# First layer: the first 512 tokens' chain moved ahead, transposes of the identity on TensorE meanwhile, and the last 512 tokens normalised on GpSimd

## The chip, the cores and the metric

The kernel runs on one core of a Trainium2 chip. It is written in Bass and Tile, as one program with instruction queues for TensorE (PE in the profile, its weight loads PEld), VectorE (DVE), ScalarE (ACT), GpSimd (POOL) and SyncE (SP, which only issues transfers here). The metric is the device time of one execution in microseconds (us), and the time of a kernel is the median of its runs.

## The reference, cut to what matters

Two layers work on 2048 tokens of width 128 in f32. Each is a layer normalisation, an attention and a gate with a residual:

```
xn = layernorm(x)                      # mean, variance, 1e-5
s  = L0_attn(xn)                       # 16 heads of width 8, relu attention
g  = silu(L0_ffn(xn))                  # 255 routed tokens go through a small block
x  = x + s * g
...                                    # layer 1: causal softmax attention, gated feed-forward
```

The relu attention of layer 0 is

```
qkv = xn @ w_qkv                       # 128 -> 16 heads x (q, k, v) of 8
w   = relu(q @ k^T / sqrt(8));  attn = w / (sum(w) + 1e-6)
out = attn @ v @ w_out + b_out;  y = xn + out;  layernorm(y) * gamma + beta
```

The routed block scores every token with `xn @ router_w`, takes the 255 highest of 2048, and works on these alone. All of it starts from the layer normalisation of the 2048 tokens, which the change touches.

## The kernel before, in words

*Tokens.* The 2048 tokens lie as 16 blocks of 128 partitions in `xin` (lines 82 to 86). They are handled in four groups of 512, and 512 is also the width of a chunk of queries. `normalised(i)` (lines 874 to 903) is a generator for one group. Its first part takes the statistics of four blocks on DVE (two instructions for each block), adds 1e-5 and takes the root on ACT; its second part forms the reciprocal root on DVE (a reciprocal and four small operations), normalises four blocks into `xne` on DVE (line 895), transposes them on TensorE into one PSUM bank (`transposed`, line 102) and copies the bank to `xnT` on ACT (line 104).

*Projections.* `project` (line 783) makes four copies of the heads' rows for one group of heads: a product `xnT` x weights, written as one 512-wide f32 product, which shows as two matmuls; a copy `high` on ACT rounded to fp32r; and a DVE instruction (line 793) that writes the rounded value or the remainder, by row, into `kT` or `qT`. This is called the split below. `spread` (line 807) does the same for all 16 heads at once, into two tiles, `high` and `low`, with one PSUM bank, tag "x", that is freed by DVE's split (line 819). These tiles go to `kT` and through DRAM (`rows`) to the other head groups by transfers on SP (`key_group`, `kept`, `group`; lines 825 to 839). `values(i)` (line 862) makes four products for v, which show as eight matmuls, and one copy on ACT.

*Steps.* The attention runs over 256 steps, n = 0 to 255: four chunks of queries, four groups of four heads, sixteen blocks of keys. `scores(n)` (line 942) makes four products side by side in the rows of the array, each into a PSUM bank of tag "s" (six of them), and four relus out of them, on ACT (line 956) or DVE (line 958), whichever `work` holds to be less loaded; `work` is a running sum of estimated microseconds for both engines. `products(n)` (line 961) comes two steps later and multiplies the relus with the values, four f32 products of two matmuls each. A step on TensorE is `scores(n)`, then what the step before left for later, then `products(n - 2)`, then one piece of other work: the piece that the table `due` (line 1066) has for the step, or else the next piece of the generator `others`, which runs the routed block first.

*Order.* TensorE, ACT and DVE issue in the order in which the program emits their instructions (`tc.manual_schedule`, line 89). GpSimd and SP are ordered by the scheduler of Tile, by emission order among what it takes to be ready. `begin` (line 907) is the part before the steps: the first parts of groups 0 and 1, the rest of group 0, `keys(0)`, the rest of group 1, `queries()`, the statistics of group 2, `values(0)`. Groups 2 and 3 are finished by `more` in steps 1 and 4.

*GpSimd.* It makes the identity matrix `ident`, re-lays the weights of the projections (lines 127 to 147), and then the constants of the routed block (lines 167 and 247 to 317): iotas, masks, zeros. Their emission stands in the first piece of the routed block, in step 10, but the scheduler puts them as early as their inputs allow. One of them, `nothing`, is 256 KB of zeros, which SP writes four times to the DRAM tile `back` (line 304). `w_qkv`, `w_out` and `router_w` are loaded on the ACT queue, all other inputs on SP's.

## Time and profile before

| | |
|---|---|
| median of 3 runs | 1464.82 us (1464.33 to 1466.9) |
| the profiled execution | 1466.11 us, its span 1464.4 us |
| busy: PE, DVE, ACT, POOL | 1412.4, 1057.6, 955.1, 329.8 us |
| mean granted TensorE clock | 0.993 |
| first transposes of tokens (line 102) | 11.27 us |
| scores of steps 0, 5, 12 (line 948) | 19.23, 36.04, 55.58 us |
| constants on POOL (lines 167 to 317) | 6.67 to 13.48 us, one more at 13.98 |

Times inside the profile count from the start of the span. A row of a timeline reads: start, length, engine, line, operation, what it writes and from what, the number of instructions merged, and in brackets how long the engine was idle before it and what ended that. A row of a table of stretches gives, behind the length, the busy time of PE, PEld, DVE, ACT and POOL with the number of instructions begun, then the granted TensorE clock as a share of the full one, the busy share of the DMA engines, and GB/s.

### The profile page before, as it was taken

The page shows a single profiled execution, that of the slowest core. Times are in us where ns is not written, and L with a number is a line of the kernel's source. Part 1 is how long each engine was busy: PE and PEld are TensorE (multiplying, and loading weights), DVE is VectorE, ACT ScalarE, POOL GpSimd, SP SyncE. Part 2 cuts the span into 40 slices and gives each one's busy share as a digit, 9 for nine tenths or more (in the row PEclk, how much of TensorE's full clock was granted, in tenths as well). Part 3 has the DMA queues.
Part 4 walks back from the last instruction along what each step waited for, and adds up shares of the span by engine and source line. Part 5 has one row for each costly group of instructions (what it writes and reads, how often), then busy time and mean ns, then how long its engine had stood idle before and what let it go on. Part 6 is the DMA issues. An engine that isn't in the chain of part 4 may idle for free.

```text
span 1464.4 us, 27046 instructions
## 1 busy us (share of the span) xinstructions
PE 1412.4 (96%) x10250; PEld 863.5 (59%) x10250; DVE 1057.6 (72%) x1905; ACT 955.1 (65%) x2055; POOL 329.8 (23%) x457
## 2 busy tenths in 40 slices
PE   5999999999999999999999999999999999999997
PEld 2222332322222476777777777777777777777775
DVE  6588788788888485577677677667667667776765
ACT  4587788788888467656556556556656656655653
POOL 2001000150000132322322222332242242242310
PEclk9999999999999999999999999999999999999999
DMA  4342001101000310010001000010010001000000
GB/s 122 122 83 69 12 12 32 51 26 42 19 20 4 99 30 15 15 30 15 16 19 24 17 16 15 17 29 16 15 30 15 15 15 30 15 15 15 16 23 23
DMA packets 33986, 44.49 MB, mean 30 GB/s; under 512 B 7360, under 2 KB 22080, under 8 KB 33856
## 3 DMA queue, kind: packets, MB, share of 16 engines
q1 hardware_dynamic: 33040, 41.45, 11.6%
q8 instruction: 81, 1.33, 0.4%
q0 software_dynamic: 384, 1.05, 0.3%
q14 instruction: 49, 0.40, 0.1%
q10 hardware_dynamic: 432, 0.26, 0.1%
HBM read 15.95 MB, written 8.17 MB: 16 GB/s over the span
## 4 chain that ended last, share of the span: by engine, by line
PE 61%; ACT 2%; DVE 1%; issue 1%; DVEq 0%; ACTq 0%
PE t L1458 18%; PE z L1508 17%; PE t L1688 16%; PE m L1568 2%; PE m L1396 2%; PE m L1361 2%; PE m L1411 2%; PE m L1553 2%; ACT p L1492 1%; ACT pt L1695 1%; PE m L1290 0%; DVE tops L1479 0%; PE m L1308 0%; DVE t L1478 0%; DVE pt L1695 0%
## 5 line engine op out<-in xcount | busy, mean ns | idle before, releaser
L1479 DVE TENSOR_REDUCE tops<-t 128x1 f32<-128x1024 f32 (+4 forms) x320 | 334.6, 1062 | 63.1 <-PE t L1458 56.0
L956 ACT ACTIVATE rt<-t 128x512 f32<-128x512 f32 x597 | 315.4, 605 | 64.7 <-PE t L948 63.3
L1695 ACT COPY pt<-t 128x512 f32<-128x512 f32 (+3 forms) x359 | 163.3, 518 | 267.1 <-PE t L1688 266.0
L1492 ACT ACTIVATE p<-t,tops 128x1024 f32<-128x1024 f32 (+7 forms) x384 | 331.0, 881 | 2.9 <-DVE tops L1479 2.4
L958 DVE TENSOR_SCALAR rt<-t 128x512 f32<-128x512 f32 x427 | 275.7, 684 | 70.0 <-PE t L948 64.9
L1458 PE MATMUL t<-k,q 128*128 128x512 f32 (+4 forms) x1280 | 316.6, 390 | 7.4 <-ACT p L1492 7.4
L964 PE MATMUL t<-rt,va 128*9 128x512 f32 x2048 | 270.0, 600 | 4.3 <-ACT part L980 4.3
L1688 PE MATMUL t<-ident,p 128*128 128x128 f32 x2176 | 269.9, 274 | 3.0 <-ACT x L1382 1.4
L1508 PE MATMUL z<-pt,v 128*64 128x256 f32 (+1 forms) x2304 | 270.0, 376 | 0.5 <-ACT zs L1702 0.5
L1458 PEld LDWEIGHTS t<-k,q 128*128 128x128 f32 x1280 | 219.1, 189 | 79.5 <-issue 36.1
L1688 PEld LDWEIGHTS t<-ident,p 128*128 128x128 f32 x2176 | 243.6, 141 | 25.4 <-ACT pt L1695 4.9
L1508 PEld LDWEIGHTS z<-pt,v 128*64 128x64 f32 x2304 | 152.6, 137 | 87.7 <-issue 23.0
L948 PEld LDWEIGHTS t<-qT,kT 32*128 32x128 f32 x1024 | 63.0, 182 | 180.8 <-ACT rt L956 108.6
L1695 DVE COPY pt<-t 128x512 f32<-128x512 f32 (+3 forms) x289 | 163.5, 605 | 2.6 <-PE z L1508 1.5
L948 PE MATMUL t<-qT,kT 32*128 32x512 f32 x1024 | 152.6, 499 | 2.7 <-ACT rt L956 1.9
L1478 DVE TENSOR_TENSOR t<-t,mask_q 128x128 f32<-128x128 f32 (+1 forms) x192 | 65.0, 339 | 86.4 <-PE t L1458 78.0
L1384 POOL CAST q<-x 64x512 fp32r<-64x512 f32 x60 | 36.6, 610 | 372.7 <-ACT x L1382 339.9
L1492 ACT ACTIVATION_READ_ACCUMULATOR p<-t,tops 128x1 f32 x384 | 84.2, 219 | 0.0
L1558 DVE TENSOR_TENSOR zs<-zs,m 128x512 f32<-128x512 f32 (+1 forms) x49 | 32.7, 675 | 65.8 <-PE m L1553 65.7
L1386 POOL TENSOR_TENSOR k<-x,k 64x512 fp32r<-64x512 f32 x60 | 76.4, 1273 | 4.6
L1386 POOL TENSOR_TENSOR q<-x,q 64x512 fp32r<-64x512 f32 x60 | 76.2, 1270 | 4.6
L1384 POOL CAST k<-x 64x512 fp32r<-64x512 f32 x60 | 36.6, 609 | 158.6 <-ACT x L1382 156.8
(316 smaller groups left out, 991.8 us busy)
## 6 DMA issues: line engine op xcount, KB each, us to landing
q<-q SPq DMA_DIRECT2D x64, 256.0 KB
qT<-spread SPq DMA_DIRECT2D x60, 64.0 KB
kT<-spread SPq DMA_DIRECT2D x48, 64.0 KB
spread<-high SPq DMA_DIRECT2D x8, 256.0 KB
spread<-low SPq DMA_DIRECT2D x8, 256.0 KB
rows<-xne SPq DMA_DIRECT2D x1, 1048.0 KB
xin<-in_x SPq DMA_DIRECT2D x4, 256.0 KB
back<-nothing SPq DMA_DIRECT2D x4, 256.0 KB
```

The lines of the kernel that those rows point to most:

```text
L948: nc.tensor.matmul(t, kT[rows, g, kb * P : (kb + 1) * P], qTs[qc, g][rows, :], start=True, stop=True,)
L956: nc.scalar.activation(rt, t, AF.Relu, scale=scale)
L958: nc.vector.tensor_scalar(rt, t, scale, 0.0, ALU.mult, ALU.max)
L964: nc.tensor.matmul(acc[32 * j : 32 * j + HD0 + 1, :], va[:, kb, 4 * g + j, :], r[j], start=(kb == 0), stop=(kb == NC - 1),)
L1384: nc.gpsimd.tensor_copy(high, x[half(e), :])
L1386: nc.gpsimd.tensor_tensor(low, x[half(e), :], high, ALU.subtract)
L1458: nc.tensor.matmul(flat[:, at_x : at_x + y - x], q[:, part, c4 * P : (c4 + 1) * P], k[:, x:y], start=(part == 0), stop=(part == 1),)
L1479: nc.vector.tensor_reduce(M[pr, c // 4][:, h, c % 4, es], x, axes, ALU.max, negate=True)
L1492: nc.scalar.activation(dst, x, AF.Exp, bias=M[pr, c // 4][:, h, c % 4, e : e + 1], accum_out=Z[pr, c // 4][:, h, c % 4, e : e + 1],)
L1508: nc.tensor.matmul(l1.z[half(e), slot, lo:2, :], V[pr, h][:, kb, half(e)], pts[e][:, kb, lo:2, :], start=(kb == 0), stop=(kb >= n0 - 1), s ...
L1688: nc.tensor.transpose(t[:, k + b, :], x[lo + b], ident)
L1695: copy(dst, t)
```

## The change

Loads: the first 512 tokens are fetched in two transfers, then `w_qkv`, then the other three groups, all on SP, where `w_out` and `router_w` are now issued too. The queries' weights are re-laid ahead of the keys'.

`normalised` is taken apart into `stats` (any blocks of a group), `root`, `normal` (on a given engine) and `turn` (transposes and copy). `fill(n)` transposes the identity n times into a PSUM bank that nobody reads. `begin` is 36 such transposes, the chain of group 0, six more transposes, queries before keys, and group 1; the key split of the first 128 keys comes by itself, ahead of that of the other 384. Only one block of group 2 has its statistics taken here.

In the steps, group 2's other statistics and normalisation follow the keys of group 1, group 3's statistics come in step 2, and group 3 is normalised by GpSimd. The table `due` is filled anew: steps 0 to 11 are all taken, so the routed block's first piece, with GpSimd's constants, comes in step 12; `rwb`, the broadcast router weight, is made there too. The reads of head group 1's keys follow the new order. GpSimd issues in emission order from `begin` to step 16.

```diff
-    for i in range(NQ):
-        nc.sync.dma_start(out=xin[:, 4 * i : 4 * i + 4, :], in_=xsrc[:, 4 * i : 4 * i + 4, :])
+    for i in range(2):
+        nc.sync.dma_start(out=xin[:, 2 * i : 2 * i + 2, :], in_=xsrc[:, 2 * i : 2 * i + 2, :])
...
-    nc.scalar.dma_start(
+    nc.sync.dma_start(
         out=w_qkv.rearrange("p g j t d -> p (g j t d)"), in_=a["w_qkv"]
     )
+    for i in range(1, NQ):
+        nc.sync.dma_start(out=xin[:, 4 * i : 4 * i + 4, :], in_=xsrc[:, 4 * i : 4 * i + 4, :])
...
-    for t, dst in ((1, w_k), (0, w_q)):
+    for t, dst in ((0, w_q), (1, w_k)):
...
-    nc.scalar.dma_start(out=w_out, in_=a["w_out"])
+    nc.sync.dma_start(out=w_out, in_=a["w_out"])
...
-    nc.scalar.dma_start(out=router_w, in_=a["router_w"])
+    nc.sync.dma_start(out=router_w, in_=a["router_w"])
...
-    nc.gpsimd.tensor_copy(rwb, router_w.to_broadcast([P, P]))
...
     yield
 
+    nc.gpsimd.tensor_copy(rwb, router_w.to_broadcast([P, P]))
     tok = rb.tile([P, KSEL], BF16, name="tok")
...
-    def project(dst, w, i, low):
+    def project(dst, w, i, low, cuts=(0, 512)):
...
-        nc.scalar.copy(high, t)
+        parts = [slice(*x) for x in zip(cuts, cuts[1:])]
+        for x in parts:
+            nc.scalar.copy(high[:, x], t[:, x])
         work.add(a=0.6, d=0.75)
-        return lambda: nc.vector.scalar_tensor_tensor(dst, high, low, t, ALU.mult, ALU.add)
+
+        def split(x):
+            nc.vector.scalar_tensor_tensor(
+                dst[:, x], high[:, x], low, t[:, x], ALU.mult, ALU.add
+            )
+
+        return [lambda x=x: split(x) for x in parts]
...
+    def stats(i, ks):
         st = small.tile([P, 4, 6], F32, tag="ln_st", name="ln_st")
+        for k in ks:
+            nc.vector.bn_stats(st[:, k, :], xin[:, 4 * i + k, :])
+            nc.vector.bn_aggr(moment[:, i, k, :], st[:, k, :])
+
+    def root(i):
...
+        nc.vector.tensor_scalar(v, moment[:, i, :, 1], 1e-5, None, ALU.add)
+        nc.scalar.activation(y, v, AF.Sqrt)
+        inverse[i] = v, y
+
+    def normal(i, engine):
...
         nc.vector.reciprocal(y, y)
+        engine.tensor_tensor(t, y, y, ALU.mult)
+        engine.tensor_tensor(t, t, v, ALU.mult)
+        engine.tensor_scalar(t, t, -0.5, 1.5, ALU.mult, ALU.add)
+        engine.tensor_tensor(r, y, t, ALU.mult)
+        for k in range(4):
+            c = 4 * i + k
+            engine.tensor_scalar(
+                xne[:, c, 0:D], xin[:, c, :], moment[:, i, k, 0:1], r[:, k : k + 1],
                 ALU.subtract, ALU.mult,
             )
...
+    def fill(n):
+
+        t = bank([P, 4, P], "s")
+        for k in range(n):
+            nc.tensor.transpose(t[:, k % 4, :], ident, ident)
 
     def begin():
 
-        next(tokens[0])
-        next(tokens[1])
-        next(tokens[0])
-        k = keys(0)
-        next(tokens[1])
-        q = queries()
-        k()
-        next(tokens[2])
-        q()
-        values(0)
-        work.a, work.d = 0.0, 3.0
+        fill(36)
+        stats(0, range(4))
+        root(0)
+        stats(1, range(2))
+        normal(0, nc.vector)
+        turn(0)
+        fill(6)
+        stats(1, range(2, 4))
+        root(1)
+        (q,) = queries()
+        k_first, k_rest = keys(0, (0, P, 512))
+        stats(2, range(1))
+        normal(1, nc.vector)
+        turn(1)
+        q()
+        k_first()
+        values(0)
+        k_rest()
+        work.a, work.d = 0.0, 1.0
+
+    def more(i):
+        turn(i)
+        work.add(a=0.6)
+        if i == 2:
+            return lambda: moments_used(3, nc.gpsimd)
+
+    def moments_used(i, engine):
+        root(i)
+        normal(i, engine)
+        work.add(a=0.2, d=0.5)
 
     def more_keys():
-        return keys(1)
+        (k,) = keys(1)
+
+        def later():
+            k()
+            stats(2, range(1, 4))
+            moments_used(2, nc.vector)
+            work.add(d=2.8)
+
+        return later
+
+    def no_more():
+        work.add(d=1.7)
+        return lambda: stats(3, range(4))
...
-        0: (more_keys,), 1: (more, 2), 2: (all_keys, 2), 3: (more_values, 1), 4: (more, 3),
-        5: (all_keys, 3), 6: (more_values, 2), 7: (all_keys, 1), 8: (all_queries, 0),
-        9: (more_values, 3), 11: (all_keys, 0),
+        0: (more_keys,), 1: (no_more,), 2: (more_values, 1), 3: (more, 2),
+        4: (all_keys, 2), 5: (more_values, 2), 6: (more, 3), 7: (all_keys, 3), 8: (all_keys, 0),
+        9: (all_queries, 0), 10: (more_values, 3), 11: (all_keys, 1),
...
-        9: (2, 1), 10: (3, 1), 12: (1, 1), 14: (0, 1),
+        9: (2, 1), 11: (3, 1), 12: (0, 1), 14: (1, 1),
...
+    first = ExitStack()
+    first.enter_context(tc.manual_schedule(engines={mybir.EngineType.Pool}))
     begin()
     for n in range(n_steps + 2):
+        if n == 16:
+            first.close()
```

## The prediction

> **What bounds the kernel now.** I read the page first: shares, slices, chain.

> ```profile
> PE 1412.4 (96%) x10250; PEld 863.5 (59%) x10250; DVE 1057.6 (72%) x1905; ACT 955.1 (65%) x2055; POOL 329.8 (23%) x457
> ...
> PE   5999999999999999999999999999999999999997
> ...
> PE 61%; ACT 2%; DVE 1%; issue 1%; DVEq 0%; ACTq 0%
> ```

> TensorE is busy 96% of the span and 5 tenths only in the first slice, so the room is in the first 40 us or so, and the wait list of TensorE from 60 to 480 us has hardly 10 us in it: what the front gains, the end should gain. Next came the timeline of the first 60 us (start, length, engine, line):

> ```profile
> 4.75 0.29 DVE L884 BATCH_NORM_STATS2 ln_st<-xin 128x6 f32<-128x128 f32 x1 [1.99 <-DMA xin<-in_x]
> ...
> 8.35 0.58 DVE L889 RECIPROCAL y<-y 128x4 f32<-128x4 f32 x1
> ...
> 10.10 1.60 DVE L895 TENSOR_SCALAR xne<-xin,ln_mv,ln_r 128x128 f32<-128x128 f32 x4
> ...
> 11.27 1.08 PE L102 MATMUL t<-ident,xne 128*128 128x128 f32 x4 [11.27 <-POOL fields L289]
> ...
> 12.39 0.58 ACT L104 COPY xnT<-t 128x512 f32<-128x512 f32 x1 [3.23 <-PE t L102]
> ...
> 13.12 2.05 PE L786 MATMUL t<-xnT,w_k 128*128 128x512 f32 x2 [0.77 <-ACT xnT L104]
> ...
> 18.43 0.75 DVE L793 SCALAR_TENSOR_TENSOR qT<-high,low_q,t 128x512 fp32r<-128x512 f32 x1
> ...
> 19.23 0.51 PE L948 MATMUL t<-qT,kT 32*128 32x512 f32 x4 [0.42 <-DVE qT L793]
> ...
> 24.50 1.15 PE L102 MATMUL t<-ident,xne 128*128 128x128 f32 x4 [2.62 <-DVE xne L895]
> ```

> One chain runs to the first scores at 19.23: load, statistics, normalisation, transposes, projections, split. In it TensorE is idle until 11.27 and then slow: a two-pass product takes 2.05 us (13.12), later 1.12 (43.53). Steps are the score rows L948: step 0 at 19.23, step 5 at 36.04, step 12 at 55.58. The third view is the table of stretches, cut where the clock changes (after the busy columns: granted clock, DMA share, GB/s):

> ```profile
> 11.18:14.59 3.41, 2.55 (x6) 1.40 (x7) 3.24 (x12) 0.58 (x1) 2.27 (x12) 1.00 1.02 276
> 21.42:24.83 3.41, 0.79 (x3) 0.43 (x3) 3.01 (x11) 2.37 (x5) 0.00 (x0) 1.00 0.00 0
> 24.83:28.24 3.41, 3.41 (x16) 0.89 (x15) 1.92 (x11) 1.86 (x5) 0.00 (x0) 0.50 0.00 0
> 31.66:35.07 3.41, 1.76 (x15) 0.45 (x13) 2.67 (x11) 1.57 (x3) 0.00 (x0) 1.00 0.64 215
> 35.07:38.48 3.41, 3.41 (x16) 0.96 (x15) 1.20 (x3) 2.16 (x4) 0.00 (x0) 0.50 0.37 97
> 523.17:526.58 3.41, 1.35 (x12) 1.11 (x10) 3.31 (x7) 2.79 (x12) 3.20 (x4) 1.00 0.03 7
> 574.37:577.78 3.41, 2.03 (x19) 1.57 (x19) 2.63 (x4) 3.39 (x8) 1.06 (x2) 1.00 0.00 0
> ```

> The clock changes on a 3.41 us grid: after stretches with 0.79, 1.76 and 1.35 us of TensorE it falls to 0.50, after full ones it is back. The two half-clock stretches follow waits for the normalisation of tokens 1024.. and 1536... Before the first change the column reads 1.00, but the 2.05 us at 13.12 shows the half clock; it goes at about 18.0.

> **The change, part by part.**

> *Loads.* The first 512 tokens come as two transfers, and w_qkv leaves the ACT queue for third place on SP's. Now 448 KB (first tokens and w_qkv together) are moved by about 3.9 (half-microsecond stretches: 128, 205, 352, 347, 344 GB/s from 2.0) and DVE starts at 4.75, some 0.9 later. Then 128 KB are moved by 2.85, 256 by 3.3: DVE starts at 3.7, with the second half at 4.2; w_qkv lands at 4.8, the next tokens at 5.4. Bounds for the start: 3.3 to 4.75 (no gain); I take 3.7, the byte count. The other moved loads (w_out, router_w; later tokens on SP) are read only after 6 us or much later. Each SP issue costs about 0.5 us. Cost nothing, as DVE covers it; uncovered, a late w_qkv (after 9.3) would hold the queries one for one.

> *First chain.* Statistics of four blocks 1.72 (4.75 to 6.47): done 5.4. Only two blocks of the next tokens stand ahead of the normalisation, 0.8 instead of 1.6: it starts at 6.3 instead of 8.35. It took 3.3 us here (8.35 to 11.70) beside POOL's constants; undisturbed (23.00 to 25.12) 2.1. Constants gone, it ends at 8.4, transposes at 9.25, the copy at 10.1.

> *TensorE kept running.* 36 transposes from 1.7 (ident is ready at 1.43). Four at half clock took 1.06, a spacing of 0.21; at full clock eight took 1.04 (574.23), 0.11. All at half clock they end at 9.3; with the clock up at this execution's grid point of 7.8, at 8.5; at that of 4.4, at 7.1. They hide under DVE's 8.4 except in the first case, by 0.9. TensorE's start has no row before 11.24; bounds 1.5 and 11.24. I take 1.7, because the other engines' first rows are at 0.3 to 2.4; at 11.24 the front would lose about 6.5 us. At full clock: queries and keys 1.06 each from 10.2, transposes of the second 512 (DVE done 12.5) to 12.9, values 1.08: first scores at 13.96. The query split (13.25) and the first 128 keys (0.3 us, 13.55) are done. **19.23 becomes 13.96: -5.3.**

> The trace has no lone run of transposes that raises the clock, but one that holds it: 574.37 to 577.78 has 2.03 us of TensorE, all of line 1688, a transpose, and the clock stays 1.00, while 1.76 us at 31.66 lost it. So I take transposes as counted.
> [...]

> *Steps 0 to 11.* I carried the four queues forward with the durations of the rows: scores 0.44, products 0.98, projection 1.06, transposes 0.58, values 1.08 on TensorE; relu 0.545 and copy 0.58 on ACT; relu 0.645, split 0.7, block statistics 0.40, normalisation 2.1 on DVE. Carried so, the present order has step 12 at 55.7 (trace: 55.58). New order: step 5 at 26.3, step 12 at 44.8. Steps 0 to 4 last 12.3 us instead of 16.8: DVE (six relus 3.9, seven block statistics 2.8, splits and a normalisation 3.5) and ACT (fourteen relus 7.6, four copies 2.3) are nearly full, TensorE no longer waits for transposes of unfinished tokens. **-4.5.** Steps 5 to 11 are TensorE's: seven bare steps of 1.42 (72.33 to 73.74 is one), four projections 4.2, two values 2.2 and transposes 0.6 are 16.9, and 1.6 of waits for the one PSUM bank of spread projections makes 18.5 instead of 19.5: the half clock at 35.07 goes (some 1.3), but spread projections now stand at 7, 8 and 9, so one more wait for DVE's split (1.0 at 47.09) comes in. **-1.0.** The router product that stood in step 10 is still owed: **+1.1.**

> *Normalisation of the last 512 on GpSimd.* It waits for DVE's reciprocal at 26.2; queued behind it are all the constants. Four small operations (0.20 each, spaced 0.28) and four of 0.61 (L714: two in 1.21) end at 30.2, just when step 6 wants its transposes. Bounds for the 0.61: 0.29 (POOL's 128x128 copy) and 1.28 (L745, four times the elements): -0 and +2.7. I take 0.61, the same operation and size.

> *Constants behind it.* Some 6.6 us of POOL, now from 30 to 37, beside steps 6 to 9. The relu of DVE is 0.627 to 0.693 in all 427 rows, with POOL busy around 296 to 325 too; the small SBUF operations were slowed (reciprocal 0.58 for 0.17, 128x128 normalisation 0.40 for 0.28). Bounds 0 and +2.8 (what both first chains lost); I take **+0.5**, two splits at that ratio. The router's broadcast weight, first in that queue, is read at step 12 only. The zero fill (4 issues, 2.33 us on SP, 1 MB) comes after its memset, near 35: its place among SP's key transfers is the scheduler's. Cost nothing: step 8 (33.3) needs keys whose split ends at 28.1, issue 1.2 and landing about 2 later.

> Sum: -5.3 -4.5 -1.0 +1.1 +0.5 = -9.2. From the profiled execution's 1466.11 (span 1464.4, 1.7 around it) that is 1456.9; it lies 1.3 above the median of the runs, which I forecast from: 1464.82 - 9.2 = **1455.6**. Own range 1453 to 1458.5: the landing (1.05), the clock's grid (a later fall costs up to 1.7 each, as at 164.8, 526.6 and 1444.8), POOL's 2.7.

> **The rivals.**
> (a) *Transposes don't raise the clock.* For: at 11.18 to 14.59, 2.55 us with transposes in it did not raise it. Against: 574.37. The first full stretch of products then ends near 18; step 0 at 18.8, step 12 at 49.7: 4.9 later, 1460.5.
> (b) *The front gain is partly given back*: GpSimd late (2.7) and the constants at their full price (2.8): about 1460.6. For: step 6 has no slack. Against: nothing else in the trace waits for POOL there.
> (c) *No change*: the step loop is held by the key transfers, so the earlier chain is waited away. For: at 65.87 scores waited 0.36 for kT<-spread. Against: that chain (split 58.1, write, read) took 8 us for group 0 and has 17 in the new order. Time 1464.
> (d) *Slower*: SP gets the zero fill ahead of the key transfers of step 5. It then waits for POOL's memset, 35.1; fill issues end 37.4, key issues 39.7, landing 42.5 or, behind the 1 MB at 315 GB/s and spread writes, up to 46. Step 8 (33.3) waits 9.2 to 12.7, and the clock falls once more (1.7): net +1.7 to +5.2, 1466.5 to 1470. It decides once those keys land after 40.8. Against: they are emitted seven steps ahead of the fill.

> **How the numbers follow.** The sum as it stands 0.62, (a) 0.14, (b) 0.13, (c) 0.05, (d) 0.06. The range must leave out no more than 2 in 10: 1452.5 (landing 3.3, a clock fall less) to 1461.5, above (a) and (b). A measurement of this kernel can tell about 0.2%, 2.9 us: faster 0.89, same 0.06 ((c), a little of (d)), slower 0.05.

> **What would show it.** Right: first scores near 14, step 5 near 26, step 12 near 45, no 0.50 clock after 8 us up to there, the first normalisation at 2.1 us, POOL's four normalisation rows near 0.6, and the rest of the trace shifted whole. Wrong: transposes near 0.21 apart to the end of the 36 and a two-pass product of 2 us after them (a); step 6 waiting for POOL (b); step 8 waiting for DMA (d); a gain at step 12 that is gone by 480 us.

## The result, and the profile after

| | before | after |
|---|---|---|
| median of 5 runs | 1464.92 us (1464.33 to 1466.9) | 1455.22 us (1453.34 to 1457.66) |
| span of the profiled execution | 1464.4 us | 1453.6 us |
| mean granted TensorE clock | 0.993 | 0.997 |
| scores of steps 0, 5, 12, 16 | 19.23, 36.04, 55.58, 65.87 us | 12.99, 25.46, 44.76, 56.59 us |

The changed kernel is faster by 9.7 us, a ratio of 0.9929 (0.9914 to 0.9943). The prediction said 1455.6.

The page of the changed kernel: busy shares, the slices of PE, the chain that ended last.

```profile
PE 1415.1 (97%) x10292; PEld 870.0 (60%) x10292; DVE 1056.7 (73%) x1900; ACT 954.5 (66%) x2054; POOL 333.9 (23%) x465
...
PE   9999999999999989999999999999999999999997
...
PE 61%; DVE 2%; ACT 2%; issue 1%; DVEq 0%; ACTq 0%
```

TensorE has 42 more instructions (10250 became 10292), which are the transposes of the identity, and its first slice went from 5 tenths to 9. A full slice means little by itself, since 7.6 of its 36 us are the idle transposes; what counts is when the first scores start. That is in the timeline of the changed kernel (start, length, engine, line):

```profile
1.48 6.76 PE L928 MATMUL t<-ident 128*128 128x128 f32 x36 [1.48 <-POOL ident masks.py:199]
...
3.04 0.29 DVE L892 BATCH_NORM_STATS2 ln_st<-xin 128x6 f32<-128x128 f32 x1 [0.28 <-DMA xin<-in_x]
...
6.07 0.15 DVE L906 RECIPROCAL y<-y 128x4 f32<-128x4 f32 x1
...
7.23 1.11 DVE L913 TENSOR_SCALAR xne<-xin,moment,ln_r 128x128 f32<-128x128 f32 x4
...
8.08 0.64 PE L102 MATMUL t<-ident,xne 128*128 128x128 f32 x4
...
9.49 1.10 PE L789 MATMUL t<-xnT,w_q 128*128 128x512 f32 x2
...
11.69 0.74 DVE L800 SCALAR_TENSOR_TENSOR qT<-high,low_q,t 128x512 fp32r<-128x512 f32 x1
...
12.99 0.50 PE L994 MATMUL t<-qT,kT 32*128 32x512 f32 x4
```

Every link of the chain is earlier or shorter. DVE starts at 3.04 instead of 4.75. From the reciprocal to the end of the normalisation are 2.27 us (6.07 to 8.34) instead of 3.35. The transposes of the tokens take 0.64 instead of 1.08, and the two-pass projection 1.10 instead of 2.05: lengths that the kernel before has where its clock column reads 1.00 after a fall (0.66 for four transposes at 60.63 us, 1.12 for a product at 43.53). Further on, in TensorE's timeline of the same kernel:

```profile
30.16 0.33 PE L102 MATMUL t<-ident,xne 128*128 128x128 f32 x1 [0.24 <-POOL xne L913]
...
35.47 1.13 PE L821 MATMUL t<-xnT,w_ka 128*128 128x512 f32 x2 [1.10 <-DVE low L830]
...
44.76 0.50 PE L994 MATMUL t<-qT,kT 32*128 32x512 f32 x4
...
47.32 1.10 PE L329 MATMUL x<-xnT,rwb 128*128 128x512 f32 x2 [1.09 <-DVE low L830]
...
56.59 0.51 PE L994 MATMUL t<-qT,kT 32*128 32x512 f32 x4 [1.23 <-DMA kT<-spread]
```

The last 512 tokens, normalised on GpSimd, kept TensorE waiting 0.24 us at step 6; the bank of the spread projections kept it 1.10 us at step 8 and 1.09 at step 12, where the router's product stands behind a spread projection (1.10 there in the kernel before); and step 16 waits 1.23 us for a key transfer. SP's timeline of the same kernel tells what stood ahead of that transfer:

```profile
34.92 0.38 SPq L307 DMA_DIRECT2D back<-nothing  x1
...
49.68 2.09 SPq L307 DMA_DIRECT2D back<-nothing  x3
51.81 8.28 SPq L843 DMA_DIRECT2D kT<-spread  x12
```

Three of the four zero writes are issued from 49.68 to 51.77, directly ahead of twelve key transfers.

Followed by the starts of the same step in both kernels, the gain is 6.24 us at step 0, 10.58 at step 5, 10.82 at step 12, 9.28 at step 16. Up to step 64 it moves between 8.3 and 10.5, since the routed block's pieces no longer fall on the same steps. Near 165 us the execution before loses 1.5 to 1.8 us to a clock fall (a stretch in which the granted clock is 0.50, here 164.78 to 168.19) that the execution after doesn't have; from step 128 on the gain is mostly between 9.3 and 10.1, and at the last copy of the attention (481.15 and 471.76 us) it is 9.39. From there both run the same work to the end, 983.25 and 981.84 us. Most of these 1.41 us is one transfer, the bias `b_K`, issued 5.37 and 5.38 us behind that copy: ScalarE could use it 5.52 us after its issue before, and 4.22 after. The changed kernel's ScalarE:

```profile
481.36 1.38 ACT L1426 ACTIVATE k<-m,b_k 64x512 fp32r<-64x512 f32 x2 [3.67 <-DMA b_k<-in_b_K]
```

and that of the kernel before:

```profile
492.04 1.38 ACT L1375 ACTIVATE k<-m,b_k 64x512 fp32r<-64x512 f32 x2 [4.96 <-DMA b_k<-in_b_K]
```

### The profile page after: what moved, and what is told of

Its sections match the earlier page's. It is cut to its first block, busy times and chain, and to the rows that moved or that the text cites. A ratio compares the mean times of both kernels' runs of the same rounds, so it can differ in the third digit from the quotient of the medians.

```text
span 1453.6 us, 27137 instructions
## 1 busy us (share of the span) xinstructions
PE 1415.1 (97%) x10292; PEld 870.0 (60%) x10292; DVE 1056.7 (73%) x1900; ACT 954.5 (66%) x2054; POOL 333.9 (23%) x465
## 3 DMA queue, kind: packets, MB, share of 16 engines
q0 software_dynamic: 384, 1.05, 0.3%
## 4 chain that ended last, share of the span: by engine, by line
PE 61%; DVE 2%; ACT 2%; issue 1%; DVEq 0%; ACTq 0%
PE t L1509 18%; PE z L1559 17%; PE t L1739 16%; PE m L1619 2%; PE m L1447 2%; PE m L1412 2%; PE m L1462 2%; PE m L1604 2%; ACT p L1543 1%; ACT pt L1746 1%; DVE tops L1530 1%; PE m L1341 0%; DVE t L1529 0%; DVE pt L1746 0%; PE m L1359 0%
```

## The experiments

Each is a change of one thing in the changed kernel unless it says otherwise. The table gives the starts of three steps and the time; the ratio is to the kernel before, run beside it on the same chip. The changed kernel itself stands first, and a second time as "after_again".

| kernel | step 0 | step 12 | step 16 | median (range), us | ratio (95%) |
|---|---|---|---|---|---|
| changed kernel | 12.99 | 44.76 | 56.59 | 1455.22 (1453.34 to 1457.66) | 0.9929 (0.9914 to 0.9943) |
| after_again | 13.33 | 44.70 | 56.77 | 1455.10 (1453.61 to 1455.22) | 0.9922 (0.9908 to 0.9935) |
| no_fill | 14.88 | 45.73 | 57.42 | 1459.39 (1458.26 to 1460.21) | 0.9954 (0.9939 to 0.9969) |
| fill_20 | 14.03 | 45.42 | 58.19 | 1456.51 (1455.00 to 1457.28) | 0.9936 (0.9919 to 0.9952) |
| fill_alone | 18.04 | 54.48 | 64.56 | 1463.17 (1459.09 to 1464.77) | 0.9984 (0.9972 to 0.9995) |
| loads_before | 14.04 | 45.82 | 57.57 | 1455.56 (1455.23 to 1457.85) | 0.9931 (0.9914 to 0.9948) |
| old_order | 12.95 | 47.60 | 58.86 | 1459.31 (1456.63 to 1460.76) | 0.9956 (0.9939 to 0.9974) |
| last_on_dve | 13.24 | 44.39 | 54.91 | 1453.46 (1452.12 to 1453.74) | 0.9911 (0.9891 to 0.9930) |
| pool_free | 14.04 | 45.53 | 55.99 | 1451.81 (1451.36 to 1452.88) | 0.9901 (0.9882 to 0.9920) |
| pool_free_again | 14.13 | 45.54 | 56.00 | 1454.11 (1453.58 to 1456.83) | 0.9923 (0.9910 to 0.9937) |
| zeros_after | 13.15 | 44.60 | 55.13 | 1454.61 (1453.23 to 1457.10) | 0.9928 (0.9911 to 0.9944) |
| queries_early | 13.45 | 44.04 | 54.07 | 1454.27 (1453.11 to 1454.69) | 0.9917 (0.9903 to 0.9930) |
| queries_early_free | 13.60 | 44.38 | 54.40 | 1453.94 (1452.29 to 1456.23) | 0.9920 (0.9907 to 0.9934) |

after_again differs from the first execution of the same kernel by 0.34 us at step 0 and 0.18 at step 16. Smaller differences than these carry nothing. The 0.34 comes from a transfer: VectorE waits 0.69 us for the next tokens in after_again and 0.23 in the first execution, and starts their statistics at 5.57 and 5.25.

**Do the idle transposes raise the clock?** Three kernels.

```diff
# no_fill
-        fill(36)
         stats(0, range(4))
...
-        fill(6)
         stats(1, range(2, 4))
```

> The changed kernel without its 42 transposes of the identity. Theory (the fill is there for the clock, and the clock is worth its price only until the first full stretch of products): the first token transposes stay near 8.1 us, because DVE sets them, but they and the first products run at half clock: queries and keys 1.75 us each instead of 1.06, values up to 2.1. Step 0 at 15.5 us (12.99 with the fill), step 12 at 47 (44.76), time about 1457.7, 2.5 above the changed kernel. Rival (a) of the prediction, price 4.9: step 12 at 49.7, time 1460. Second rival: the clock comes up by itself in time, step 0 within 0.5 us of 13.0.

TensorE's timeline of no_fill:

```profile
7.69 1.15 PE L102 MATMUL t<-ident,xne 128*128 128x128 f32 x4 [7.69 <-DVE xne L913]
...
9.60 2.05 PE L789 MATMUL t<-xnT,w_q 128*128 128x512 f32 x2 [0.77 <-ACT y L899]
11.44 1.92 PE L789 MATMUL t<-xnT,w_k 128*128 128x512 f32 x2
...
14.88 0.51 PE L992 MATMUL t<-qT,kT 32*128 32x512 f32 x4
```

Without the 42 transposes the queries start at 9.60, where the changed kernel has 9.49, and each of the two projections takes 1.9 to 2.05 us instead of 1.1. So it is the clock and not the order that the transposes pay for: 1.89 us at step 0. At step 12 only 0.97 is left, and 0.83 from step 16 to the fall at 157 us. Of what is given back by step 12, 0.41 lies in steps 0 to 4, where the changed kernel has a half-clock stretch (17.12) that no_fill doesn't have; beside after_again, which has none either, nothing is given back there (1.55 us at step 0, 1.54 at step 5). The other 0.51 lies in steps 5 to 11, where two of the changed kernel's waits, 0.24 and 0.20 us, are missing. The 4.9 us that rival (a) put on it at step 12 is not there. The median is 4.2 us above the changed kernel's, which 0.83 doesn't explain. In the profiled execution of no_fill the rest can be followed: a clock fall at 157 us (1.5), a wait for GpSimd at 422 (0.73), a longer wait of ScalarE at 485 (by its place again for the bias `b_K`, though the row names a product), which holds TensorE 1.03 us longer at 487, and a clock fall at 488 (1.7), from which the difference in the falls near 525 us takes some 1.7 off again. All five of its runs are above every run of the changed kernel. Clock falls alone can't be why: two of the five have a mean granted clock of 0.998, as the best runs of the changed kernel do, and took 1458.26 and 1460.21 us. What held those two is left open.

```diff
# fill_20
-        fill(36)
+        fill(20)
```

> The changed kernel with 20 transposes of the identity ahead instead of 36. They end near 5.8 us, so no stretch of the 3.41 us grid is full. Theory (a full stretch is needed): the clock stays at half as without the fill, queries 1.75 us, step 0 at 14.5 to 15. Rival (any activity of two thirds of a stretch will do, or the phase of the grid decides): queries 1.06 us and step 0 at 13.0.

The timeline and a table of stretches of fill_20 (after the length: busy PE, PEld, DVE, ACT, POOL; then the granted clock, DMA share, GB/s):

```profile
1.48 4.25 PE L928 MATMUL t<-ident 128*128 128x128 f32 x20 [1.48 <-POOL ident masks.py:199]
7.61 1.10 PE L102 MATMUL t<-ident,xne 128*128 128x128 f32 x4 [1.88 <-DVE xne L913]
...
9.65 1.91 PE L789 MATMUL t<-xnT,w_q 128*128 128x512 f32 x2
```

```profile
8.50:11.40 2.90, 2.90 (x10) 1.86 (x11) 2.59 (x15) 0.79 (x2) 0.00 (x0) 0.54 0.52 104
```

Twenty transposes end at 5.73 and TensorE is idle for 1.88 us. The granted clock of the stretch behind it is 0.54, the queries take 1.91, and step 0 comes 1.04 later than with 36. The clock had risen here too and was lost again: in the trace the transposes start 0.21 us apart up to 5.2 us and the last one 0.11 behind the one before it, and the six that follow those of the tokens start 0.11 us apart at 8.6 and 0.21 from 8.8 us on. So the expectation, that 20 would leave it at half, failed, and 14.03 lies between its 14.5 to 15 and the rival's 13.0; step 0 is still 0.85 earlier than without any. With twenty transposes and 1.88 us of idleness behind them the clock was lost before the queries; with 36, which the chain's own work followed without a wait, it wasn't. What share of a stretch TensorE has to be busy, all of it or two thirds, these runs don't show. (The 1.60 at step 16 has 0.94 of another kind: TensorE waits 2.17 us for keys there, 1.23 in the changed kernel.)

```diff
# fill_alone: the kernel before, with this in begin, ahead of next(tokens[0])
+        t = bank([P, 4, P], "s")
+        for n in range(36):
+            nc.tensor.transpose(t[:, n % 4, :], ident, ident)
```

> The kernel before with 36 transposes of the identity ahead of its first part and nothing else changed. Theory: the fill ends near 8.2 us and the first token transposes come at 11.3 as before, so one stretch of the clock's 3.41 us grid has only about 1.2 us of TensorE in it and the clock falls again: step 0 near 19.2, step 12 near 55.6, time 1465, no change. Rival (the fill alone is what warms the first products): queries and keys at 1.06 us, step 0 at 17.4, time 1463.

TensorE's timeline of fill_alone:

```profile
1.48 6.69 PE L911 MATMUL t<-ident 128*128 128x128 f32 x36 [1.48 <-POOL ident masks.py:199]
9.98 0.59 PE L102 MATMUL t<-ident,xne 128*128 128x128 f32 x2 [1.81 <-DVE xne L895]
...
12.45 1.10 PE L786 MATMUL t<-xnT,w_k 128*128 128x512 f32 x2 [0.77 <-POOL fields L289]
...
14.53 1.92 PE L786 MATMUL t<-xnT,w_q 128*128 128x512 f32 x2
```

The old front with the transposes has its keys at the full clock (1.10) and its queries at half (1.92): the clock fell at 13.55, after the idle gaps that the longer chain leaves (1.81, 0.67 and 0.77 us). It gains 1.19 us at step 0, 1.10 at step 12 and 1.31 at step 16. The theory said no change and the rival 17.4 for step 0; the truth, 18.04, lies between. The transposes are worth something by themselves, and more (1.89 at step 0) with a front short enough to follow them without gaps.

**The loads.** The first 512 tokens as one transfer again, `w_qkv`, `w_out` and `router_w` on the ACT queue.

```diff
# loads_before
-    for i in range(2):
-        nc.sync.dma_start(out=xin[:, 2 * i : 2 * i + 2, :], in_=xsrc[:, 2 * i : 2 * i + 2, :])
+    for i in range(NQ):
+        nc.sync.dma_start(out=xin[:, 4 * i : 4 * i + 4, :], in_=xsrc[:, 4 * i : 4 * i + 4, :])
...
-    nc.sync.dma_start(
+    nc.scalar.dma_start(
         out=w_qkv.rearrange("p g j t d -> p (g j t d)"), in_=a["w_qkv"]
     )
-    for i in range(1, NQ):
-        nc.sync.dma_start(out=xin[:, 4 * i : 4 * i + 4, :], in_=xsrc[:, 4 * i : 4 * i + 4, :])
...
-    nc.sync.dma_start(out=w_out, in_=a["w_out"])
+    nc.scalar.dma_start(out=w_out, in_=a["w_out"])
...
-    nc.sync.dma_start(out=router_w, in_=a["router_w"])
+    nc.scalar.dma_start(out=router_w, in_=a["router_w"])
```

> The changed kernel with the loads of the kernel before: four transfers of 512 tokens on SP, w_qkv, w_out and router_w on the ACT queue. Theory (the early start is the loads' doing): DVE's first statistics at 4.75 us instead of 3.04, and everything to step 12 later by 1.0 to 1.7; step 0 at 14.0 to 14.7, step 12 at 45.8 to 46.5, time 1 to 1.7 more. Rival (the first step is held elsewhere, by TensorE's fill or the queries' weights): step 0 later by less than 0.5.

DVE's timeline of loads_before:

```profile
4.58 0.29 DVE L890 BATCH_NORM_STATS2 ln_st<-xin 128x6 f32<-128x128 f32 x1 [1.81 <-DMA xin<-in_x]
```

DVE starts 1.54 later (4.58 against 3.04) and step 0 comes 1.05 later, step 12 1.06, step 16 0.98: the new loads are worth about 1 us at each. Beside after_again it is 0.71 at step 0. In the median it is 0.3, less than the runs of either kernel scatter, where 1 to 1.7 was expected.

**The order of the steps.** The new front with the old tables; the statistics of group 3 stand with those of group 2.

```diff
# old_order
-            work.add(d=2.8)
+            stats(3, range(4))
+            work.add(d=4.5)
...
-        0: (more_keys,), 1: (no_more,), 2: (more_values, 1), 3: (more, 2),
-        4: (all_keys, 2), 5: (more_values, 2), 6: (more, 3), 7: (all_keys, 3), 8: (all_keys, 0),
-        9: (all_queries, 0), 10: (more_values, 3), 11: (all_keys, 1),
+        0: (more_keys,), 1: (more, 2), 2: (all_keys, 2), 3: (more_values, 1), 4: (more, 3),
+        5: (all_keys, 3), 6: (more_values, 2), 7: (all_keys, 1), 8: (all_queries, 0),
+        9: (more_values, 3), 11: (all_keys, 0),
...
-        9: (2, 1), 11: (3, 1), 12: (0, 1), 14: (1, 1),
+        9: (2, 1), 10: (3, 1), 12: (1, 1), 14: (0, 1),
```

> The changed kernel, its new front kept, with the table of steps of the kernel before (and the statistics of the last group taken with the second last). Theory (steps 0 to 11 are shorter because of the new order): from step 0 to step 12 they last 35 us or more, as in the kernel before (36.35), against 31.8 in the changed kernel; with the router's first product back in step 10 the net loss is 2 to 3.5 us, time 1457.5 to 1458.5. Rival (the shorter steps come from the new front alone, since most statistics are taken earlier): 32 to 33 us, time within 1 of the changed kernel.

TensorE's timeline of old_order:

```profile
20.13 1.16 PE L102 MATMUL t<-ident,xne 128*128 128x128 f32 x4 [4.95 <-DVE xne L913]
...
44.08 1.12 PE L329 MATMUL x<-xnT,rwb 128*128 128x512 f32 x2
...
47.60 0.50 PE L995 MATMUL t<-qT,kT 32*128 32x512 f32 x4
```

With the same front (step 0 at 12.95) the old order leaves TensorE idle for 4.95 us, waiting for the normalisation of group 2, and step 12 comes at 47.60: from step 0 to step 12 pass 34.65 us instead of 31.77. Of these 2.9 us some 1.1 is the router's first product, which the old order makes in step 10 (44.08) and the changed kernel has still to make. At step 16 the new order is worth 2.3 us, from there to step 64 between 1.7 and 3.1, and in the median 4.1 (its profiled execution has a clock fall at 156.5 us too). Without it 8.0 of the 10.8 us at step 12 would still have been there.

**GpSimd's two jobs.** In the first kernel the last 512 tokens are normalised by DVE; the constants then start at 10.57, for nothing stands ahead of them in GpSimd's queue.

```diff
# last_on_dve
-            return lambda: moments_used(3, nc.gpsimd)
+            return lambda: moments_used(3, nc.vector)
```

> The changed kernel with the last 512 tokens normalised on DVE. GpSimd then has nothing ahead of its constants that waits, so they run from about 6.5 us on as in the run with GpSimd left to the scheduler. Theory (DVE is nearly full in steps 0 to 4): against that run step 0 is the same and step 6 comes 1 to 2 us later, time 1 to 2 us more. Rival (DVE has room there): steps 6 and 12 within 0.4 us of that run.

DVE does the four blocks in 1.11 us, merged, from 26.77 to 27.88, where GpSimd takes 3.14 (26.96 to 30.10), and the scores do not wait for it: step 12 comes 0.37 earlier and step 16 1.68. DVE had the room, and the move to GpSimd was not needed. The 1.68 holds a second thing: with the constants early, the memset of the zeros ends at 15.42 instead of 34.89, and step 16 doesn't wait for keys. The expectation, step 6 later than with GpSimd left to the scheduler, failed: it comes at 28.17, and at 28.96 in that run, the second kernel.

In the second kernel GpSimd is ordered by the scheduler from the start, and normalises the last 512 as in the changed kernel.

```diff
# pool_free, and again in pool_free_again
-    first = ExitStack()
-    first.enter_context(tc.manual_schedule(engines={mybir.EngineType.Pool}))
     begin()
     for n in range(n_steps + 2):
-        if n == 16:
-            first.close()
```

> The changed kernel with GpSimd ordered by the scheduler as before, so that its constants run from about 6.5 to 13 us again, beside the first two normalisations. Theory (constants slow the small SBUF operations of DVE there): the two normalisations, 2.1 us each in the changed kernel, take 2.7 to 3.3, step 0 at 14.5 to 15.2 instead of 12.99; the zero fill is out of SP's way early, so step 16 no longer waits 1.2 us for its keys; time 1455 to 1456.5. Rival (the constants were hidden): step 0 at 13.0 and the whole 1.2 us faster, 1454.

A few of the constants now lie at 7.35 to 7.81 us, beside the first chain; GpSimd then waits 2.63 us for `router_w`, and the others lie from 10.44 to 16.5, beside the second chain and behind it. The zero writes are issued at 12.07. DVE's timeline of pool_free, in the first and the second chain:

```profile
7.24 0.51 DVE L909 TENSOR_SCALAR t<-t 128x4 f32<-128x4 f32 x1
...
11.54 1.29 DVE L913 TENSOR_SCALAR xne<-xin,moment,ln_r 128x128 f32<-128x128 f32 x4
```

A small operation that takes 0.32 in the first chain of the changed kernel takes 0.51, and the second normalisation, 1.11 there, takes 1.29. From the reciprocal on the first chain lasts 2.52 us for 2.27 and the second 2.39 for 2.08 (2.50 and 2.60 in pool_free_again), not the 2.7 to 3.3 that was expected. Step 0 is 1.05 later than in the changed kernel, step 12 0.77 later, and step 16 is 0.60 earlier, because it doesn't wait for the keys. Of the 1.05, 0.56 is the slower chains and 0.49 the statistics of the next tokens, which start later for want of their transfer; as after_again waits 0.69 us for the same transfer, that part can't be put down to the constants. So the constants beside the two chains cost 0.6 us at the start (0.75 in pool_free_again), and the constants behind the normalisation cost more than that at step 16.

The median was 3.4 us below the changed kernel's, which 0.6 at step 16 doesn't explain. So both kernels were run once more, side by side.

> The changed kernel once more, on the chip of the next three, so that they can be set beside it: 1453.5 to 1457, median 1455.2 as before; step 0 within 0.5 us of 13.0, step 16 within 1 us of 56.6.

> The changed kernel with GpSimd left to the scheduler, once more beside it. Theory (the constants behind the normalisation cost more at step 16, through the zero writes, than they save before step 0): 0.6 to 2.5 us faster than the changed kernel on the same chip. Rival (the 3.4 us between the medians of the two earlier runs was the clock's later falls and the chip): within 0.5 us.

pool_free_again has the same landmarks as pool_free (14.13, 45.54, 56.00), but 1454.11 us, and after_again has 1455.10: the difference is 1.0, with ranges that overlap. Most of the 3.4 us was not of the kernel. The stretches behind 151 us show it, first in pool_free and then in pool_free_again:

```profile
151.05:154.46 3.41, 3.31 (x23) 1.42 (x23) 2.48 (x5) 3.38 (x7) 0.00 (x0) 1.00 0.12 22
154.46:157.87 3.41, 3.01 (x23) 0.73 (x23) 2.77 (x5) 3.41 (x8) 0.00 (x0) 1.00 0.01 2
```

```profile
152.15:155.56 3.41, 2.91 (x18) 0.96 (x20) 3.41 (x5) 3.40 (x8) 0.00 (x0) 1.00 0.09 17
155.56:158.97 3.41, 3.41 (x20) 0.42 (x12) 1.79 (x4) 3.31 (x8) 0.00 (x0) 0.50 0.00 0
```

The same kernel at the same place keeps its clock in one execution and loses it in the other, and the loss costs 1.5 us. It isn't only the profiled executions: the mean granted clock of pool_free's four runs is 0.997 or 0.998, and 0.995 in four of the five of pool_free_again. The fifth, with 0.998, took 1453.58 us, still 1.6 to 2.2 above the runs of pool_free with 0.998. The kernel before was 0.8 us slower on that chip (1465.8 for 1465.0); the rest is open.

**The zero writes.** The zeros are made late, from the finished row of router scores times zero, so that both the memset and the four writes come after step 16's keys.

```diff
# zeros_after
-    nc.gpsimd.memset(nothing, 0.0)
-    for i in range(NQ):
-        nc.sync.dma_start(
-            out=back[512 * i : 512 * i + 512, :].rearrange("(c p) d -> p c d", p=P), in_=nothing
-        )
...
+    nc.gpsimd.tensor_scalar(
+        nothing.rearrange("p a d -> p (a d)"), wrow[:, :512], 0.0, None, ALU.mult
+    )
+    for i in range(NQ):
+        nc.sync.dma_start(
+            out=back[512 * i : 512 * i + 512, :].rearrange("(c p) d -> p c d", p=P), in_=nothing
+        )
```

> The changed kernel with the zeros for the DRAM tile made on GpSimd from the finished router row (times 0) instead of by a memset, so that SP writes them only after step 18. Theory (in the changed kernel three of the four zero writes, 2.1 us of SP at 49.7, stand ahead of the key transfers, and step 16 waits for those): steps 0 to 15 as in the changed kernel, step 16 at 55.0 to 55.4 (56.59), no wait for a transfer there, time 1.2 to 1.6 us less, 1453.8. Rival (the wait has another cause, the key reads themselves): step 16 at 56.6 still, time unchanged.

SP's timeline of zeros_after, and then TensorE's:

```profile
47.87 4.91 SPq L845 DMA_DIRECT2D kT<-spread  x8
52.91 2.53 SPq L344 DMA_DIRECT2D back<-nothing  x4
```

```profile
55.13 0.51 PE L996 MATMUL t<-qT,kT 32*128 32x512 f32 x4
```

Eight key transfers now go at 47.87, ahead of the zeros. Step 16 starts at 55.13 with no wait for a transfer, 1.46 earlier, while step 12 is only 0.16 earlier. The wait was the zero writes'. By step 60 0.92 is left of it, and in the median 0.6, within the scatter of the runs, where 1.2 to 1.6 was expected.

**What a faster order would bring.** The spread product of the queries is moved into step 1, where the changed kernel has none, the last values to step 8, and step 10 is left to the routed block; the last 512 tokens go to DVE. The second kernel has the same table, with GpSimd ordered by the scheduler and normalising the last 512.

```diff
# queries_early
-            return lambda: moments_used(3, nc.gpsimd)
+            return lambda: moments_used(3, nc.vector)
...
+        split = all_queries(0)
...
-        0: (more_keys,), 1: (no_more,), 2: (more_values, 1), 3: (more, 2),
-        4: (all_keys, 2), 5: (more_values, 2), 6: (more, 3), 7: (all_keys, 3), 8: (all_keys, 0),
-        9: (all_queries, 0), 10: (more_values, 3), 11: (all_keys, 1),
+        0: (more_keys,), 1: (early_queries,), 2: (more_values, 1), 3: (more, 2),
+        4: (all_keys, 2), 5: (more_values, 2), 6: (more, 3), 7: (all_keys, 3),
+        8: (more_values, 3), 9: (all_keys, 0), 11: (all_keys, 1),
```

> The changed kernel with the last 512 tokens normalised on DVE, the spread projection of the queries in step 1, where TensorE waits for relus and nothing was due, the last values in step 8, and step 10 left to the routed block. Theory (steps 7 to 12 lose a us each time two spread projections stand side by side, and step 1 has TensorE time to spare): step 5 later by up to 1 us, step 12 at 43 to 43.8 (44.39 with only the DVE part changed), with the router's product of step 10 paid by then; time 1.5 to 3 us below the run with only the DVE part, 1450.5 to 1452. Rival (DVE and ACT are so full in steps 1 to 3 that the moved projection costs there what it saves later): step 12 at 44.4 or later, time within 1 of that run.

> The same order of steps, with the last 512 tokens on GpSimd as in the changed kernel and GpSimd left to the scheduler. Theory: the constants cost step 0 about 1 us as in that run, DVE has 1.9 us less in step 4; step 12 at 44 to 44.8, time 1450 to 1452. Rival: as for the run before, no gain over GpSimd left to the scheduler alone (1451.8).

Both are ahead of the changed kernel, by 2.5 and 2.2 us at step 16 and by 2.7 and 2.5 at step 64. Much of this is not the queries': last_on_dve is 1.68 ahead at both steps, so that the moved product adds 0.84 and 1.0 in the first kernel; beside pool_free it adds 1.6 and 1.7 in the second. The times of 1450.5 to 1452 and 1450 to 1452 that were expected didn't come. The medians are lower by 0.8 to 1.2 than that of the changed kernel beside them (1455.10), and the intervals of the ratios overlap its interval. In the profiled executions the rest goes in clock falls: queries_early falls at 151.96 (some 1.8 us) and at 288.5 (some 2 us), queries_early_free near 153; neither execution of the changed kernel that was profiled falls there. The other runs fit this: the mean granted clock is 0.995 or 0.996 in all five of queries_early and 0.996 to 0.998 in those of queries_early_free, and 0.997 or 0.998 in after_again's five. No version is shown to be faster than the changed kernel.

## Why the prediction was right, step by step

**Loads.** Right in kind, and the start was earlier than taken: 3.04, not 3.7, and below even the lower bound of 3.3. The term that was too cautious is the 0.9 us behind the bytes moved: by the half microseconds from 1.5 us (28, 202 and 255 GB/s) the first 128 KB were moved by about 2.6, an estimate, and DVE started some 0.5 us later.

**First chain.** Predicted to run from 6.3 to 8.4; it ran from 6.07 to 8.34. Most of DVE's earlier start was lost again: 0.25 us for the addition ahead of the root, which the working had left out, and a wait of 0.23 for the next tokens. The constants' part was argued as 1.2 us of slowing (3.3 against 2.1). In the changed kernel the chain is 1.08 shorter than it was, but pool_free, with 0.25 and 0.31 us for its two chains, doesn't show that the constants were the cause of all of it: its first normalisation runs beside none of them. How much of the old 3.35 us came from the constants is not shown.

**TensorE kept running.** Predicted step 0 at 13.96, -5.3; measured 12.99, -6.24. The mechanism is as told: the transposes started at 1.48, and they raised the clock, as the table of half-microsecond stretches of that line alone shows (after the length: busy PE and PEld, in brackets the instructions that touch the stretch; then clock, DMA share, GB/s):

```profile
5.50:6.00 0.50, 0.50 (x4) 0.50 (x3) 1.00 0.73 215
...
7.00:7.50 0.50, 0.50 (x7) 0.50 (x6) 1.00 0.59 174
```

Four or five in half a microsecond become seven near 7 us. In the trace their starts lie 0.21 us apart up to 6.9 us and 0.11 after. The clock column reads 1.00 from the start, as in the kernel before, and can't be used here; the rate can. The term was 0.9 us too small, and two pieces hold most of it: the tokens' transposes follow DVE block by block and end 0.38 us after it (0.85 was taken), and their copy needed 0.63 instead of 0.85. Rival (a) is refuted: in 1.48 to 8.24 TensorE ran transposes alone, and within them the 0.21 became 0.11. By single removal from the changed kernel, the transposes are worth 1.89 us at step 0, the loads 1.05 and GpSimd's order 1.05, each 0.34 less beside after_again; of the last, 0.56 is the constants'. These needn't add up. What remains of 6.24, 2.25 by these numbers, may be the chain's new order (two blocks of statistics ahead instead of four, queries first, the first 128 keys by themselves), which wasn't tried by itself.

**Steps 0 to 4.** Predicted 12.3 us, measured 12.47 (16.81 before): -4.34 for -4.5. One of its signs failed here. The prediction said that no half-clock stretch would come after 8 us; there is one, in the changed kernel's table of stretches:

```profile
13.70:17.12 3.42, 2.94 (x12) 0.94 (x12) 2.66 (x5) 2.93 (x6) 0.00 (x0) 1.00 0.02 3
17.12:20.50 3.38, 3.38 (x16) 1.68 (x16) 2.80 (x16) 2.06 (x5) 0.00 (x0) 0.50 0.02 5
```

It cost little. after_again has no such fall; its step 3 starts at 19.52, 1.25 earlier, but its step 5 at 25.40, 0.06 earlier, and its steps 0 to 4 last 12.07 us, 0.40 less. That the others of these steps are held by ACT and DVE, which the prediction had as nearly full, fits the two rows above (2.66 and 2.93, then 2.80 and 2.06 us busy of 3.4), but wasn't tested.

**Steps 5 to 11.** This is the term that failed in size: -1.0 predicted, -0.24 measured (19.30 us against 19.54). TensorE waits 1.10, 0.45 and 0.20 us for DVE's split of the spread projections and 0.24 for GpSimd, 1.99 in all where 1.6 was taken; the other 0.4 us is TensorE's work, 17.3 us for the 16.9 of the sum.

**Last 512 on GpSimd.** The duration was wrong, and the end was right because a second error met it. An operation takes 0.79 us (3.14 for four), not 0.61; but DVE's reciprocal let it start at 25.81 instead of 26.2, so that the last block ends at 30.10 for the predicted 30.2, and TensorE waits 0.24. Of rival (b)'s 2.7 nothing came. last_on_dve shows that DVE could have done it without loss.

**Constants behind it.** +0.5 was taken for splits slowed beside GpSimd. No such loss shows in steps 6 to 9 that the split waits above don't hold, and it wasn't measured apart.

**The zero fill at nothing** was wrong: 1.46 us at step 16. The prediction had its mechanism in rival (d), zero writes ahead of key transfers on SP, but looked only at the keys of step 8. One write did go at 34.92, as expected, without harm. The other three went at 49.68, between the last spread writes and the twelve key transfers that step 16 waits for. The sum had no row for them.

**The sum.** -6.24 - 4.34 - 0.24 is -10.82 at step 12, for -10.8 predicted there (-5.3 - 4.5 - 1.0): the front's gain was under-sized by 0.94 and that of the steps over-sized by 0.16 and 0.76. Of the later terms, the zero writes took 1.46 at step 16, 0.92 of it lasting, where the sum had 0.5 for the constants. The router product owed, +1.1, is paid by step 20: by then each kernel has run four of these products and four transposes of their row. What it cost can't be read apart: the gain swings between 8.3 and 10.5 up to step 64, and without the clock fall of the execution before, the 9.4 at the attention's end would be 7.6 to 7.9, so that some 1.4 to 1.7 us went between step 16 and there, which is near that term and wasn't traced. The total of -9.2 met -9.7 in part by errors that cancelled. Part of the hit is luck: the profiled executions differ by 10.8 us, of which 1.3 is the late bias transfer and 1.5 to 1.8 the clock fall, and no run ties either to the change. Rival (c), the gain waited away at the key transfers, is refuted in the main: of 10.82 us, 1.46 went there. Its sign, 0.36 at 65.87, was idle time of the weight loads; TensorE itself stood 0.13 us there (65.74 to 65.87).

## What to carry to other kernels

When a kernel's bound engine is idle at the start, look for what makes its first work late, and for what makes it slow: here the idle transposes alone in the old front were worth 1.2 us and the order of the steps behind the new front 2.3 at step 16. Moving an engine's work later also moves the transfers that hang on it (here three zero writes to 49.68, which cost 1.46 us at step 16), and each must be checked against everything that its queue issues from then on, not only against the next reader. And a difference of 1 to 3 us in 1455 is to be read from landmarks in the trace, such as the start of the same step: one more or less clock fall (1.5 to 1.8 us each near 160 us), or one late transfer (1.3), in an execution is as large.

## What the runs showed of the hardware

*Busy time doesn't tell a fall.* The stretch 13.70 to 17.12 of the changed kernel has 2.94 us of busy TensorE and lost the clock, and the one of after_again that answers to it (13.59 to 17.00) has 2.93 and kept it; the stretch 574.37 to 577.78 of the kernel before kept it with 2.03 us, all of transposes. The stretches that fell with 2.4 to 2.9 us hold score products, which use 32 of the 128 rows (32*128 in their timeline rows), in pieces with waits between them. What makes these stretches lose the clock and the others keep it stays open.

*GpSimd and VectorE.* A normalisation of 128x128 with two scalars of each partition takes 0.79 us on GpSimd and some 0.28 on VectorE. Beside GpSimd's work VectorE's small operations took longer. The normalisation of four blocks took 1.11 us alone and 1.29 in pool_free. One operation on 128x4 values took 0.17 alone, 0.32 beside a memset of GpSimd, 0.51 in pool_free, and 1.29 in the kernel before; in VectorE's timelines of the changed kernel (first two) and of the kernel before:

```profile
6.67 0.32 DVE L909 TENSOR_SCALAR t<-t 128x4 f32<-128x4 f32 x1
10.26 0.17 DVE L909 TENSOR_SCALAR t<-t 128x4 f32<-128x4 f32 x1
```

```profile
12.21 1.29 DVE L892 TENSOR_SCALAR t<-t 128x4 f32<-128x4 f32 x1
```

The two longer ones end at 6.99 and 13.50, 0.03 and 0.02 us behind a GpSimd memset (6.96 and 13.48). That looks like waiting for it rather than like running slower; no run tests it.
